# A two-layer graph kernel: TensorE issues in the order of the text, and the second layer multiplies by its weights before it mixes the nodes

## Chip, cores and metric

The kernel runs on one core of one Trainium2 chip. The metric is the device time of one execution in microseconds (us); the median of several runs counts. All data are float32.

## What is computed

There are 64 graphs (the batch) of 256 nodes with 512 features, and one 256 x 256 adjacency matrix for all of them. Layer 0 is masked attention with 8 heads of 64 features, layer 1 a graph attention with one head; both have a layernorm and a ReLU ahead of them and a residual around them.

```python
h = relu(layernorm(x))
q, k, v = h @ Wq + bq, h @ Wk + bk, h @ Wv + bv      # 8 heads of 64
scores = q k^T / 8 + (1 - adj) * -1e9                # per graph and head, 256 x 256
y = x + (softmax(scores) v) @ Wo + bo

h = relu(layernorm(y))
g = h @ W                                            # 512 x 512
s1, s2 = g @ a1, g @ a2                              # one number per node each
e = leaky_relu(s1[:, None] + s2[None, :], 0.2) * adj
out = y + elu(softmax(e) g + beta * g)
```

## The kernel before

Nodes lie on the 128 partitions in two tiles (`NT` = 2), features in four chunks of 128 (`DC` = 4), heads in four pairs (`NPAIR` = 4). Weights, mask and adjacency stay in SBUF. One pass of the main loop over `b` works on up to four graphs at once: the attention of graph `b`, the projections of graph `b+1`, the output projection and the second layer's scores of graph `b-1`, and the second layer's mixing and output of graph `b-2`. The text gives a priority to each step; which instruction an engine issues next was settled when the program was built, by a scheduler that may move steps past each other, and each engine then works through a fixed queue.

The steps that matter here, with the lines of the profile:

- `norm` and `norm_t` (lines 135 to 149 in their helpers): layernorm of `x`, then eight TensorE transposes (tile `tr_h`, two PSUM tiles of four), and a ReLU on the way back to SBUF, the first tile on VectorE (line 149) and the second on ScalarE (line 147).
- `project_qk` (line 184) fills one PSUM tile `qk` with a q chunk and a k chunk; VectorE takes q out (line 186), ScalarE then k (line 187). `project_v` (line 194) fills two tiles `pv`.
- `scores` (line 205): for a head pair, four matmuls with 64 rows of contraction into one tile `sc`, the heads on the two halves of the partitions. VectorE adds the mask (line 208) and takes the row maximum (line 214), ScalarE makes the exponentials with their sums (line 154), VectorE the reciprocal (line 156), GpSimd the product (line 216).
- `values`: eight transposes of the weights (tile `at`, line 163), copied to SBUF by ScalarE for the first head (line 165) and by VectorE for the second (line 167), then four matmuls (tile `av`, line 231) with 64 output columns per head: both node tiles of the first head, then both of the second. ScalarE copies the result (line 233).
- `project_o` (line 241, tiles `po`), the layernorm of `y`, with ReLU and without a transpose (line 252).
- `gat_scores`: VectorE multiplies `h` by the two vectors `W a1` and `W a2` and sums (line 262, four instructions), two small matmuls spread one of the sums over the partitions (tile `pe`, line 267); after the exponentials VectorE divides and adds `beta` on the diagonal (line 280).
- `gat_mix`: four transposes of the weights (tile `at_g`), and ((att + beta I) h) transposed, as eight matmuls of 256 columns (tiles `pz`, line 295). `gat_out`: that times W (tiles `pg`, line 307), then elu and the residual on ScalarE and VectorE, and the store.

A float32 matmul stands in the trace as two MATMUL instructions, each with its own weight load; a transpose stands as one. So `project_qk` of one chunk pair is eight matmuls and 16 instructions.

PSUM is held by three pools of two tiles each: `ps_sc` for `sc`, `ps_tr` for `at` and `at_g`, and `ps_mm` for all else (`tr_h`, `qk`, `pv`, `av`, `po`, `pe`, `pz`, `pg`). A tile of `ps_mm` can be filled only after one of the two before it has been copied out.

Of the kernel before, what the change touches and what calls it, by code (L numbers as in the profile page):

```python
# [14 lines left out]
P = 128  # L15
# [5 lines left out]
def kernel(ctx: ExitStack, tc: tile.TileContext, x, adj, wq, bq, wk, bk, wv, bv, wo, bo, w, a, beta, out):  # L21
# [23 lines left out]
    X, XN, HT, QT, KT, V, S, OT, Y, H2, ATT, ZT = ({} for _ in range(12))  # L45
# [48 lines left out]

    nc.vector.tensor_scalar(bo_sb, bo_sb, -1.0, None, ALU.add)

    diag = const.tile([P, NT, N], F32, name="diag")
    nc.gpsimd.memset(diag, 0.0)
    for t in range(NT):
        nc.vector.tensor_scalar(diag[:, t, t * P:(t + 1) * P], ident, beta_sb, None, ALU.mult)  # L100


    wa = const.tile([P, DC, 2], F32, name="wa")
    war = const.tile([P, 2, D], F32, name="war")

    def project_a():
        for j in range(2):
            aj = p2.tile([P, D], F32, tag="o", name=f"a_{j}")
            nc.sync.dma_start(aj, a[j * D:(j + 1) * D, 0].partition_broadcast(P))
            for c in range(DC):  # L110
                prod = p2.tile([P, D], F32, tag="t", name=f"prod_{j}_{c}")
                nc.vector.tensor_tensor(prod, w_sb[:, c, :], aj, ALU.mult)
                nc.vector.tensor_reduce(wa[:, c, j:j + 1], prod, AX.X, ALU.add)
            ps = ps_mm.tile([P, D], F32, tag="mm", name=f"war_{j}")
            for c in range(DC):
                nc.tensor.matmul(ps[:, c * P:(c + 1) * P], wa[:, c, j:j + 1].to_broadcast([P, P]), ident,
                                 start=True, stop=True)
            nc.vector.tensor_copy(war[:, j, :], ps)

    def statistics(src, name):  # L120

        st = p3.tile([P, NT, 6], F32, tag="st", name=f"st_{name}")
        mv = p3.tile([P, NT, 2], F32, tag="mv", name=f"mv_{name}")
        rstd = p3.tile([P, NT], F32, tag="rstd", name=f"rstd_{name}")
        for t in range(NT):
            nc.vector.bn_stats(st[:, t, :], src[:, t, :])
            nc.vector.bn_aggr(mv[:, t, :], st[:, t, :])
        nc.vector.tensor_scalar(rstd, mv[:, :, 1], EPS, None, ALU.add)
        nc.gpsimd.tensor_tensor(rstd, rstd, mhalf, ALU.pow)
        return mv, rstd  # L130

    def layernorm(src, name):

        mv, rstd = statistics(src, name)
        dst = p2.tile([P, NT, D], F32, tag="ln", name=f"ln_{name}")
# [15 lines left out]
    def exponents(e, rows, nmax, ssum):  # L151
# [4 lines left out]
        nc.vector.reciprocal(ssum, ssum)  # L156

# [42 lines left out]
    def scores(b, hp):  # L200
# [14 lines left out]
        exponents(rows, 2 * NT, nmax, ssum)  # L215
        nc.gpsimd.tensor_tensor(rows, rows, ssum.unsqueeze(2).to_broadcast([P, 2 * NT, N]), ALU.mult)  # L216
        S[b, hp] = s

    def values(b, hp):
        s = S.pop((b, hp))  # L220
        if hp == 0:
            OT[b] = p2.tile([P, NPAIR, N], F32, tag="oT", name=f"oT_{b}")
        sT = []
        for h in range(2):
            sT.append(p2.tile([P, NT, N], F32, tag="sT", name=f"sT_{b}_{hp}_{h}", bufs=4))
            transposed_weights(lambda t: s[:, h, t, :], sT[h], f"{b}_{hp}_{h}", (nc.scalar, nc.vector)[h])
        ps = ps_mm.tile([P, 512], F32, tag="mm", name=f"av_{b}_{hp}")
        for h in range(2):
            c0 = (2 * hp + h) * HD
            for k in range(NT):  # L230
# [5 lines left out]
    def project_o(b):  # L236
        Y[b] = p2.tile([P, NT, D], F32, tag="y", name=f"y_{b}", bufs=3)
        for t in range(NT):
            ps = ps_mm.tile([P, D], F32, tag="mm", name=f"po_{b}_{t}")
            for c in range(DC):  # L240
                nc.tensor.matmul(ps, OT[b][:, c, t * P:(t + 1) * P], wo_sb[:, c, :],  # L241
                                 start=(c == 0), stop=(c == DC - 1))
            nc.vector.tensor_tensor(Y[b][:, t, :], ps, X[b][:, t, :], ALU.add)
        for d in (OT, X, QT, KT, V):
            d.pop(b)

        mv, rstd = statistics(Y[b], f"y{b}")
        shift = p3.tile([P, NT], F32, tag="shift", name=f"shift_{b}")
        nc.vector.scalar_tensor_tensor(shift, mv[:, :, 0], -1.0, rstd, op0=ALU.mult, op1=ALU.mult)
        H2[b] = p2.tile([P, NT, D], F32, tag="h2", name=f"h2_{b}")  # L250
        for t in range(NT):
            nc.scalar.activation(H2[b][:, t, :], Y[b][:, t, :], AF.Relu, scale=rstd[:, t:t + 1],
                                 bias=shift[:, t:t + 1])


    def gat_scores(b):
        h2 = H2[b]
        s12 = p3.tile([P, 2, NT], F32, tag="s12", name=f"s12_{b}")
        for j in (1, 0):
            for t in range(NT):  # L260
                prod = p2.tile([P, D], F32, tag="t", name=f"sp_{b}_{j}_{t}")
                nc.vector.scalar_tensor_tensor(prod, h2[:, t, :], 1.0, war[:, j, :], op0=ALU.mult, op1=ALU.mult,  # L262
                                               accum_out=s12[:, j, t:t + 1])

        ps = ps_mm.tile([P, 512], F32, tag="mm", name=f"pe_{b}")
        for t in range(NT):
            nc.tensor.matmul(ps[:, t * P:(t + 1) * P], s12[:, 1, t:t + 1].to_broadcast([P, P]), ident,  # L267
                             start=True, stop=True)
        raw = p2.tile([P, NT, N], F32, tag="raw", name=f"raw_{b}")
        for t in range(NT):  # L270
            nc.scalar.activation(raw[:, t, :], ps[:, :N], AF.Identity, bias=s12[:, 0, t:t + 1])
# [6 lines left out]
        exponents(e, NT, nmax, ssum)  # L278
        for t in range(NT):
            nc.vector.scalar_tensor_tensor(e[:, t, :], e[:, t, :], ssum[:, t:t + 1], diag[:, t, :],  # L280
                                           op0=ALU.mult, op1=ALU.add)
        ATT[b] = e

    def gat_mix(b):

        e, h2 = ATT.pop(b), H2.pop(b)
        eT = p2.tile([P, NT, N], F32, tag="eT", name=f"eT_{b}")
        transposed_weights(lambda t: e[:, t, :], eT, f"g{b}", nc.vector)
        ZT[b] = p2.tile([P, DC, N], F32, tag="zT", name=f"zT_{b}")
        for i in range(2):  # L290
            ps = ps_mm.tile([P, 2, N], F32, tag="mm", name=f"pz_{b}_{i}")
            for j in range(2):
                c = 2 * i + j
                for k in range(NT):
                    nc.tensor.matmul(ps[:, j, :], h2[:, k, c * P:(c + 1) * P], eT[:, k, :],  # L295
                                     start=(k == 0), stop=(k == NT - 1))
            if i:
                nc.scalar.copy(ZT[b][:, 2:4, :], ps)
            else:
                nc.vector.tensor_copy(ZT[b][:, 0:2, :], ps)  # L300

    def gat_out(b):
        zT, y = ZT.pop(b), Y.pop(b)
        for t in range(NT):
            ps = ps_mm.tile([P, D], F32, tag="mm", name=f"pg_{b}_{t}")
            for c in range(DC):
                nc.tensor.matmul(ps, zT[:, c, t * P:(t + 1) * P], w_sb[:, c, :],  # L307
                                 start=(c == 0), stop=(c == DC - 1))
            m = p2.tile([P, D], F32, tag="t", name=f"m_{b}_{t}")
            nc.scalar.activation(m, ps, AF.Exp)  # L310
            nc.vector.scalar_tensor_tensor(m, m, 1.0, y[:, t, :], op0=ALU.min, op1=ALU.add)  # L311
            o = p2.tile([P, D], F32, tag="o", name=f"o_{b}_{t}")
            nc.vector.scalar_tensor_tensor(o, ps, 0.0, m, op0=ALU.max, op1=ALU.add)  # L313
            nc.sync.dma_start(out[b, t * P:(t + 1) * P, :], o)

    norm(0)
    norm_t(0)
    for d in range(DC):
        project_qk(0, d)
    project_v(0)  # L320
    scores(0, 0)
    project_a()

    for b in range(B + 2):
        prev, nxt = 0 <= b - 1 < B, b + 1 < B
        for hp in range(NPAIR):
            if b < B and hp + 1 < NPAIR:
                scores(b, hp + 1)
            if hp == 0:
                if b + 2 < B:  # L330
                    load(b + 2)
                if nxt:
                    norm(b + 1)
                if prev:
                    project_o(b - 1)
                if 0 <= b - 2 < B:
                    gat_mix(b - 2)
            elif hp == 1:
                if nxt:
                    norm_t(b + 1)  # L340
                    project_qk(b + 1, 0)
                    project_qk(b + 1, 1)
            elif hp == 2:
                if 0 <= b - 2 < B:
                    gat_out(b - 2)
                if prev:
                    gat_scores(b - 1)
                if nxt:
                    project_qk(b + 1, 2)
            else:  # L350
                if nxt:
                    project_qk(b + 1, 3)
                    project_v(b + 1)
                    scores(b + 1, 0)
            if b < B:
                values(b, hp)
# [29 lines left out]
```

## Time and profile before

| | us |
|---|---|
| median of 3 runs | 3751.84 (3750.86 to 3754.07) |
| the profiled execution's own time | 3754.07 |
| its span in the trace | 3752.3 |
| TensorE matmul busy | 3652.5 (97% of the span) |
| VectorE busy | 2137.2 (57%) |
| ScalarE busy | 1239.1 (33%) |
| GpSimd busy | 723.5 (19%) |
| share of the DMA engines in queue 1 | 5.7% |

The span runs from the first to the last instruction of the profiled execution; 1.8 us of its own time lie outside it, and this execution was 2.2 us over the median. "Busy" of TensorE counts matmuls from start to a modelled end, and they overlap, so the distance from one instruction's start to the next one's start (its pace) says more than its duration. The mean granted TensorE clock was 0.993. From the third pass of the loop on, the trace repeats itself every 57.76 us.

### The profile page before, as it was taken

To read this page: it belongs to the slowest core of one execution; us is meant where nothing else is said; L and a number is where in the kernel's file an instruction comes from. 1 tells how busy PE (TensorE), PEld (TensorE's weight loads), DVE (VectorE), ACT (ScalarE), POOL (GpSimd) and SP (SyncE) were. 2 spreads that over 40 slices of the span, in tenths; PEclk is the share of its full clock that TensorE was granted. 3 is DMA by queue.
4 is the path that set the end of the run, shared out by engine and by line. 5 is a ranking of instruction groups with operands and counts; after the bars stand their busy time and mean duration, and the time that the engine had idled before them with its cause. 6 is when DMAs were issued, how large, how long until landed. Compare 5 with 4: busy or idle time off the path is not lost.

```text
span 3752.3 us, 40118 instructions
## 1 busy us (share of the span) xinstructions
PE 3652.5 (97%) x15376; PEld 2288.7 (61%) x15376; DVE 2137.2 (57%) x3735; ACT 1239.1 (33%) x3585; POOL 723.5 (19%) x456
## 2 busy tenths in 40 slices
PE   8999999999999999999999999999999999999998
PEld 5666665666666656666566666665666656666664
DVE  5555555555555555555555555555555555555554
ACT  2333333333333333333333333333333333333332
POOL 2221121221211212212122121121221212212110
PEclk9999999999999999999999999999999999999999
DMA  2000000000000000000000000000000000000000
GB/s 99 12 20 20 17 17 17 23 17 18 17 21 19 17 17 20 20 17 17 17 23 17 18 17 23 17 17 17 23 17 17 18 17 23 17 18 17 17 12 17
DMA packets 40721, 76.24 MB, mean 20 GB/s; under 512 B 4433, under 2 KB 4689, under 8 KB 40529
## 3 DMA queue, kind: packets, MB, share of 16 engines
q1 hardware_dynamic: 40528, 73.68, 5.7%
q8 instruction: 121, 1.98, 0.2%
q14 instruction: 72, 0.58, 0.1%
HBM read 40.11 MB, written 33.55 MB: 20 GB/s over the span
## 4 chain that ended last, share of the span: by engine, by line
PE 84%; DVE 11%; ACT 4%; issue 0%; DMA 0%; POOL 0%; POOLq 0%; DVEq 0%; ACTq 0%
PE qk L184 25%; PE po L241 12%; PE pv L194 12%; PE sc L205 11%; PE av L231 9%; PE pz L295 6%; PE at L163 5%; DVE m L311 4%; ACT s L154 4%; DVE s L208 2%; DVE nmax L214 2%; PE tr_h L145 2%; PE pe L267 2%; DVE sp L262 1%; DVE o L313 1%; ACT m L310 1%
## 5 line engine op out<-in xcount | busy, mean ns | idle before, releaser
L216 POOL TENSOR_TENSOR s<-s,ssum 128x1024 f32<-128x1024 f32 x256 | 484.5, 1892 | 2742.2 <-DVE ssum L156 2694.1
L154 ACT ACTIVATE s<-s,nmax 128x256 f32<-128x256 f32 x1024 | 507.7, 497 | 683.0 <-DVE nmax L214 681.7
L208 DVE TENSOR_TENSOR s<-sc,mask 128x1024 f32<-128x1024 f32 x256 | 313.6, 1225 | 402.0 <-PE sc L205 402.0
L184 PE MATMUL qk<-hT,wq 128*128 128x256 f32 x2048 | 513.7, 395 | 2.1 <-ACT hT L147 1.6
L184 PE MATMUL qk<-hT,wk 128*128 128x256 f32 x2048 | 484.3, 379 | 0.0
L241 PE MATMUL po<-wo,oT 128*128 128x512 f32 x1024 | 456.8, 599 | 0.0
L307 PE MATMUL pg<-w,zT 128*128 128x512 f32 x1024 | 456.4, 598 | 0.0
L205 PE MATMUL sc<-kT,qT 64*128 64x256 f32 x2048 | 456.3, 422 | 0.0
L194 PE MATMUL pv<-wv,hT 128*128 128x512 f32 x1024 | 449.9, 592 | 0.0
L184 PEld LDWEIGHTS qk<-hT,wq 128*128 128x128 f32 x2048 | 385.3, 196 | 93.3 <-ACT sT L165 21.1
L184 PEld LDWEIGHTS qk<-hT,wk 128*128 128x128 f32 x2048 | 389.8, 190 | 53.4
L231 PE MATMUL av<-sT,v 128*64 128x256 f32 x2048 | 352.3, 392 | 2.7 <-ACT sT L165 1.5
L241 PEld LDWEIGHTS po<-wo,oT 128*128 128x128 f32 x1024 | 189.2, 190 | 235.5 <-issue 220.2
L307 PEld LDWEIGHTS pg<-w,zT 128*128 128x128 f32 x1024 | 189.4, 190 | 235.0 <-issue 234.8
L165 ACT COPY sT<-at 128x512 f32<-128x512 f32 x256 | 149.5, 584 | 551.3 <-PE at L163 551.1
L194 PEld LDWEIGHTS pv<-wv,hT 128*128 128x128 f32 x1024 | 194.6, 190 | 217.6 <-issue 214.3
L186 DVE TENSOR_SCALAR qT<-qk,bq 128x256 f32<-128x256 f32 x256 | 123.9, 484 | 345.9 <-PE qk L184 345.9
L205 PEld LDWEIGHTS sc<-kT,qT 64*128 64x128 f32 x2048 | 219.4, 185 | 154.9 <-issue 140.0
L214 DVE TENSOR_REDUCE nmax<-s 128x4 f32<-128x1024 f32 x256 | 311.2, 1216 | 4.3
L163 PE MATMUL at<-ident,s 128*128 128x128 f32 x2048 | 299.9, 275 | 0.9 <-POOL s L216 0.9
L163 PEld LDWEIGHTS at<-ident,s 128*128 128x128 f32 x2048 | 240.5, 141 | 96.3 <-issue 87.8
L231 PEld LDWEIGHTS av<-sT,v 128*64 128x64 f32 x2048 | 172.8, 136 | 142.6 <-issue 53.4
(63 smaller groups left out, 3299.2 us busy)
## 6 DMA issues: line engine op xcount, KB each, us to landing
x<-in_x_dram SPq DMA_DIRECT2D x64, 512.0 KB, 3.7
out_dram<-o SPq DMA_DIRECT2D x128, 256.0 KB, 2.0
wq<-in_L_gnn_Wq_dram SPq DMA_DIRECT2D x1, 1024.0 KB, 6.5
wk<-in_L_gnn_Wk_dram SPq DMA_DIRECT2D x1, 1024.0 KB, 9.1
wv<-in_L_gnn_Wv_dram SPq DMA_DIRECT2D x1, 1024.0 KB, 7.5
wo<-in_L_gnn_Wo_dram SPq DMA_DIRECT2D x1, 1024.0 KB, 9.1
w<-in_L_gnn_W_dram SPq DMA_DIRECT2D x1, 1024.0 KB, 11.4
a<-in_L_gnn_a_dram SPq DMA_DIRECT2D x2, 256.0 KB, 10.2
```

What stands on the lines that cost most here:

```text
L154: nc.scalar.activation(e[:, r, :], e[:, r, :], AF.Exp, bias=nmax[:, r:r + 1], accum_out=ssum[:, r:r + 1])
L163: nc.tensor.transpose(ps[:, k, t * P:(t + 1) * P], e(t)[:, k * P:(k + 1) * P], ident)
L184: nc.tensor.matmul(ps[:, j, :], wj[:, c, d * P:(d + 1) * P], HT[b][:, c, :], start=(c == 0), stop=(c == DC - 1))
L194: nc.tensor.matmul(ps, HT[b][:, c, t * P:(t + 1) * P], wv_sb[:, c, :], start=(c == 0), stop=(c == DC - 1))
L205: nc.tensor.matmul(ps[:, h, t, :], QT[b][hs, hp, t * P:(t + 1) * P], KT[b][hs, hp, :], start=True, stop=True)
L208: nc.vector.tensor_tensor(s.rearrange("p h t k -> p h (t k)"), ps.rearrange("p h t k -> p h (t k)"), mask.rearrange("p t k -> p (t k)").un ...
L214: nc.vector.tensor_reduce(nmax, rows, AX.X, ALU.max, negate=True)
L216: nc.gpsimd.tensor_tensor(rows, rows, ssum.unsqueeze(2).to_broadcast([P, 2 * NT, N]), ALU.mult)
L231: nc.tensor.matmul(ps[h * HD:(h + 1) * HD, :N], V[b][:, k, c0:c0 + HD], sT[h][:, k, :], start=(k == 0), stop=(k == NT - 1))
L241: nc.tensor.matmul(ps, OT[b][:, c, t * P:(t + 1) * P], wo_sb[:, c, :], start=(c == 0), stop=(c == DC - 1))
L295: nc.tensor.matmul(ps[:, j, :], h2[:, k, c * P:(c + 1) * P], eT[:, k, :], start=(k == 0), stop=(k == NT - 1))
L307: nc.tensor.matmul(ps, zT[:, c, t * P:(t + 1) * P], w_sb[:, c, :], start=(c == 0), stop=(c == DC - 1))
```

## The change

TensorE's queue now follows the text: the main part stands inside a manual schedule for that engine, and the loop body is written out as the list in which TensorE is to work. The other engines are still scheduled at build time. `values` is split into `weights_t` (the transposes and their copies) and `values` (the matmuls), with other work between the two; the matmuls of `values` alternate between the heads. The score matmuls of a head pair, which alternated before, stay together.

The second layer is evaluated in another order. The layernorm of `y` is now transposed as that of `x` is (`gat_norm_t`, tiles `tr_g`, eight transposes), and `gat_h` makes g = h W (tiles `ph`, 16 instructions of 512 columns, copied to SBUF by ScalarE). The two score terms come from the transposed `h` on TensorE: `W a2`, spread over 128 columns (`wa2b`), gives one term with four matmuls of 256 columns, and eight matmuls with a single moving column give the other. The weights are divided on GpSimd, as in layer 0, without the diagonal. `gat_out` needs two matmuls of 512 columns per tile; beta times g is added by VectorE, and elu takes two passes on ScalarE and three on VectorE. `project_a` and the constants lose what is not needed any more.

```diff
-        for h in range(2):
-            c0 = (2 * hp + h) * HD
-            for k in range(NT):
+        for k in range(NT):
+            for h in range(2):
+                c0 = (2 * hp + h) * HD
                 nc.tensor.matmul(ps[h * HD:(h + 1) * HD, :N], V[b][:, k, c0:c0 + HD], sT[h][:, k, :],
                                  start=(k == 0), stop=(k == NT - 1))
...
+    def gat_norm_t(b):
+        H2T[b] = p2.tile([P, DC, N], F32, tag="h2T", name=f"h2T_{b}")
+        transposed_relu(YN.pop(b), H2T[b], f"g{b}")
+        HS[b] = p2.tile([P, NT, D], F32, tag="hs", name=f"hs_{b}")
+    def gat_h(b, t):
+        ps = ps_mm.tile([P, D], F32, tag="mm", name=f"ph_{b}_{t}")
+        for c in range(DC):
+            nc.tensor.matmul(ps, H2T[b][:, c, t * P:(t + 1) * P], w_sb[:, c, :],
+                             start=(c == 0), stop=(c == DC - 1))
+        nc.scalar.copy(HS[b][:, t, :], ps)
     def gat_scores(b):
...
+        for c in range(DC):
+            nc.tensor.matmul(ps[:, :N], wa2b[:, c, :], h2T[:, c, :], start=(c == 0), stop=(c == DC - 1))
+        for t in range(NT):
+            for c in range(DC):
+                nc.tensor.matmul(ps[:, N + t:N + t + 1], h2T[:, c, t * P:(t + 1) * P], wa[:, c, 0:1],
                                  start=(c == 0), stop=(c == DC - 1))
...
     def gat_out(b):
...
-            for c in range(DC):
-                nc.tensor.matmul(ps, zT[:, c, t * P:(t + 1) * P], w_sb[:, c, :],
-                                 start=(c == 0), stop=(c == DC - 1))
+            for k in range(NT):
+                nc.tensor.matmul(ps, eT[:, k, t * P:(t + 1) * P], hs[:, k, :],
+                                 start=(k == 0), stop=(k == NT - 1))
+            nc.vector.scalar_tensor_tensor(g, hs[:, t, :], beta_sb, ps, op0=ALU.mult, op1=ALU.add)
-            nc.scalar.activation(m, ps, AF.Exp)
+            nc.scalar.activation(m, g, AF.Relu, scale=-1.0)
+            nc.scalar.activation(m, m, AF.Exp, scale=-1.0)
...
+    with tc.manual_schedule(engines={mybir.EngineType.PE}):
```

The order of TensorE's queue in one full pass (`b` the graph whose attention is worked on), as the built program has it:

| graph b | graph b+1 | graph b-1 | graph b-2 |
|---|---|---|---|
| sc 1 | | po 0 | |
| at 0 | | po 1 | at_g |
| av 0 | tr_h 0, 1 | | pg 0, 1 |
| sc 2 | qk 0 | | |
| at 1 | qk 1 | | |
| av 1, sc 3 | | tr_g 0, 1 | |
| | qk 2 | | |
| at 2 | | ph 0 | |
| av 2 | | ph 1, pe, 16 single-column instructions | |
| | sc 0 | | |
| at 3 | qk 3 | | |
| av 3 | pv 0, 1 | | |

Rows follow each other, and within a row TensorE goes from left to right. Of the two PSUM tiles of `ps_mm`, pg 0 takes the one that tr_h 0 filled and pg 1 that of tr_h 1; qk 2 takes that of tr_g 1, ph 0 that of tr_g 0, pv 0 that of qk 3, and av 3 that of `pe`. VectorE's queue in the same pass has, behind the scores of graph b-1, this order: copy of s1, leaky ReLU, product with adj, mask of sc 0 (b+1), row maximum of e, row maximum of sc 0, copy of at 3 (second head), reciprocals, q of qk 3. ScalarE's has: two `raw`, copy of at 3 (first head), exponentials of e, exponentials of sc 0, k of qk 3, copy of av 3.

## The prediction

> **What bounds the kernel now.** I read the page first. TensorE is busy 97% of the span, and 84% of the chain that ended last lies on it.
>
> ```profile
> PE 3652.5 (97%) x15376; PEld 2288.7 (61%) x15376; DVE 2137.2 (57%) x3735; ACT 1239.1 (33%) x3585; POOL 723.5 (19%) x456
> PE 84%; DVE 11%; ACT 4%; issue 0%; DMA 0%; POOL 0%; POOLq 0%; DVEq 0%; ACTq 0%
> ```
>
> So TensorE's queue sets the time: what it issues, at what pace, and what it waits for. The waits, next, show one real wait of it in each batch:
>
> ```profile
> PE pe L267 <- DVE sp L262: 72.1, 64, 1.8
> ```
>
> For the pace I take the timeline of TensorE in the middle of the run: start, length of the group, line, tiles, count. A group's cost is the distance to the next group's start, since lengths overlap.
>
> ```profile
> 1800.98 7.03 PE L194 MATMUL pv<-wv,hT 128*128 128x512 f32 x16
> ...
> 1811.45 7.13 PE L241 MATMUL po<-wo,oT 128*128 128x512 f32 x16
> 1818.42 0.60 PE L163 MATMUL at_g<-ident,e 128*128 128x128 f32 x4
> ...
> 1820.02 3.72 PE L295 MATMUL pz<-eT,h 128*128 128x256 f32 x16
> 1823.58 0.60 PE L163 MATMUL at<-ident,s 128*128 128x128 f32 x4
> 1824.15 1.89 PE L231 MATMUL av<-sT,v 128*64 128x256 f32 x8
> 1825.97 0.70 PE L205 MATMUL sc<-kT,qT 64*128 64x256 f32 x4
> 1826.60 1.09 PE L145 MATMUL tr_h<-ident,ln_x 128*128 128x128 f32 x8
> ...
> 1836.23 1.09 PE L231 MATMUL av<-sT,v 128*64 128x256 f32 x8
> 1837.25 1.13 PE L205 MATMUL sc<-kT,qT 64*128 64x256 f32 x6
> 1838.31 7.13 PE L307 MATMUL pg<-w,zT 128*128 128x512 f32 x16
> 1845.28 0.93 PE L163 MATMUL at<-ident,s 128*128 128x128 f32 x7
> 1847.33 0.49 PE L267 MATMUL pe<-ident,s 128*128 128x128 f32 x2 [1.13 <-DVE sp L262]
> ```
>
> The next pv begins at 1858.73, 57.75 us later: the batch's period (57.76 on average). Single instructions inside these groups start 0.429 us apart for 512 columns, 0.216 for 256, 0.109 for a transpose. The same eight av instructions cost 1.02 us at 1836.23 and 1.82 at 1824.15, where the copies of the transposed weights came late; a piece of four sc costs 0.63, of six 1.06, and the unbroken eight of the prologue (at 33.80) also 1.06.
>
> [...] an `at` is followed after 0.202 us by an sc instead of 0.109, the last sc or av of a group takes 0.306 instead of 0.216, and the first full-array instruction after it 0.104 more (0.056 for a transpose). [...] in the av at 1836.23 the second head's first matmul, queued behind four instructions of the first head, starts 13 ns after that head's first. So the heads already overlap, and alternating them in the text buys nothing by itself.
>
> **The change, part by part, per batch.** *Taken off TensorE:* pz 16 x 0.216 = 3.46; half of pg, 8 x 0.429 = 3.43; the two old pe with their wait, 0.74 + 1.29. Scores: nine pieces cost 6.57, four unbroken groups 4 x 1.064 = 4.26: -2.32. Values: the four groups cost 1.82 + 1.28 + 2 x 1.02 = 5.15; with other matmuls between transposes and values all can run at 1.02: -1.06. Mode changes around the groups, counted in both lists: -0.10. Together -12.40. *Added:* ph 16 x 0.429 = 6.86; the new pe 8 x 0.216 = 1.73; tr_g 8 x 0.109 = 0.87; 16 single-column instructions, which the trace does not show. Each loads 128 weight columns, [...] not over the 0.213 that the old pe takes from first to second instruction with its load exposed; I take the load-bound pace of the transposes, 0.109: 1.74. Together +11.21. Work alone: 57.76 - 12.40 + 11.21 = 56.57, a gain of 1.19.
>
> *Waits added.* TensorE may no longer slip other work in, so each late copy stops all behind it. I laid the batch out along the fixed queues with these durations (mean ns of one):
>
> ```profile
> L154 ACT ACTIVATE s<-s,nmax 128x256 f32<-128x256 f32 x800 | 396.7, 497 | 541.0 <-DVE nmax L214 541.0
> L216 POOL TENSOR_TENSOR s<-s,ssum 128x1024 f32<-128x1024 f32 x200 | 378.5, 1892 | 2168.2 <-DVE ssum L156 2168.2
> L208 DVE TENSOR_TENSOR s<-sc,mask 128x1024 f32<-128x1024 f32 x200 | 245.0, 1225 | 322.6 <-PE sc L205 322.6
> L311 DVE SCALAR_TENSOR_TENSOR m<-m,y 128x512 f32<-128x512 f32 x100 | 149.6, 1496 | 15.1 <-ACT m L310 15.1
> L149 DVE TENSOR_SCALAR hT<-tr_h 128x512 f32<-128x512 f32 x50 | 34.0, 681 | 0.0
> L147 ACT ACTIVATE hT<-tr_h 128x512 f32<-128x512 f32 x50 | 29.9, 599 | 64.2 <-PE tr_h L145 64.2
> ```
>
> From TensorE coming free to the reader's start the trace has 0.20 us, from a copy's end to TensorE 0.05; independent neighbours on VectorE or ScalarE overlap by 0.09.
> 1. pg 0 needs the PSUM tile of tr_h 0: 0.20 + 0.68 + 0.04 = 0.92 after tr_h 0, covered by tr_h 1 alone (0.44): 0.48. Before, transposes and scores stood behind tr_h.
> 2. qk 2 needs the tile of tr_g 1, straight ahead of it: 0.20 + 0.60 + 0.05 = 0.85, no cover.
> 3. av 3 needs the second head's copy on VectorE, queued behind graph b-1's second-layer scores. From pe's end: s1 0.41, two `raw` on ScalarE 0.91, leaky ReLU 0.73, product 0.60, mask of sc 0 1.14, maximum of e 0.60, maximum of sc 0 1.14, the copy with its landing 0.72: 6.25. Cover: sc 0 1.06, at 3 0.93, qk 3 3.55: 5.54. Wait 0.71.
> 4. pv 0 needs qk 3's tile; its k copy stands on ScalarE behind the four exponentials of sc 0 (1.99, 0.49 apart). They start 5.66 after pe's end, the copy takes 0.52: 8.17. Cover 5.54 + 0.71 + 1.02 = 7.27. Wait 0.90.
> 5. Behind waits 1 and 2 the weight load cannot run ahead: 2 x 0.104 = 0.21.
>
> Sum 3.15. Period 56.57 + 3.15 = 59.72, against 57.76: +1.96.
>
> *At no cost:* softmax chains have 14 us or more of other matmuls (about 7.5 needed); the layernorm of y 16 us (about 7). VectorE loses four products and the division and gains copies and elu steps, and stays near 60%; ScalarE gains two copies and two passes. GpSimd gains the second layer's product (about 0.95, half of 1.89), between graphs' softmax products, with 12 us to spare. SP's loads and stores are the same in number and size, and queue 1 moves in 5.7% of the time. One cover is thin: av 1 has 0.34 us to spare behind the elu, mask and exponentials of sc 2. [...] the trace shows an `m` (line 311) lasting 2.31 us instead of 0.69, ending 0.55 after a GpSimd product. The new elu step meets GpSimd's addition to x (2.35 us). That costs 0 to 0.1; if the layernorm scaling is caught too, 0.7.
>
> **The sum.** The profiled execution's span is 3752.3. Its 61 full batches: 61 x 1.96 = +119.6. Ends, laid out the same way: the prologue loses the matmuls that spread a (line 116) but must keep the text's order, about -1.5. The second pass lacks only at_g and pg (3.9), so 55.8; before it lacked pz and a longer pg too, and took 47.3 from po to po: +8.5. The pass of the last graph, without graph b+1, 38.5 against 35.4: +3.1. From the last po on: po 7.0, at_g with its copy and pg 4.9, tr_g with its copies 1.8, ph 6.9, pe 3.5, the score chain to the product 5.9, at_g with copy 1.4, pg 3.4, last elu, store and end 7.4, so 42.2 against 47.1: -4.9. Together +5.2. Every fifth or sixth batch has 1.64 us at half TensorE clock; I leave it. 3752.3 + 124.8 = 3877.1; with 1.8 outside the span 3878.9 for that execution, and 2.2 less on the median: 3876.7.
>
> **Rivals.** *The copies keep ahead.* With the same two `ps_mm` tiles the profile of before has scarcely a wait of TensorE but pe's, which speaks for readers that are always in time. With 0.5 us of waits left per batch the period would be 57.07: 61 x -0.69 + 5.2 gives 3715. It decides for faster once the waits sum to under 1.1 us (1.19 less the ends' 5.2 / 61). Against it: before, other matmuls stood between tr_h and the next user of its tile, and waits 1 and 2 alone make 1.33 out of measured durations. *VectorE is later still*[...]: av 1 waits 0.7 more, 61 x 0.7 = 43, 3919. *The single-column instructions expose their loads* (0.213): +1.66 a batch, 3978. *The change does not do what it says:* for the values this holds, as said, and is in the sum.
>
> **Chances.** Forecast (3825 to 3905) 0.60; [...] exposed loads 0.09; faster 0.07; balance within 0.2% (7.5 us, about what a measurement of this kernel can tell from no change) 0.04. Slower is 0.60 + 0.20 + 0.09 = 0.89. The range 3825 to 3950 leaves out faster, balance and exposed loads, 0.20.
>
> **What would show it.** The period between two pv should be 59.7; sc groups of eight at 1.06, av at 1.02; single-column starts 0.109 apart; TensorE idle ahead of pg (released by VectorE hT), qk 2 (ScalarE h2T), av 3 (VectorE sT) and pv 0 (ScalarE kT). I am wrong if those idle times are under half of what I list, or if others as large appear.

## The result and the profile after

| | before | after |
|---|---|---|
| median | 3752.76 (3750.86 to 3754.07, 4 runs) | 3856.97 (3856.38 to 3857.76, 4 runs) |
| ratio, 95% interval | | 1.0278 [1.026, 1.0296] |
| the profiled execution's own time | 3754.07 | 3856.66 |
| its span | 3752.3 | 3854.9 |
| period in the middle of the run | 57.76 | 59.53 |

The change costs 2.8%. The page's first part and its chain, after:

```profile
PE 3707.5 (96%) x16640; PEld 2315.6 (60%) x16640; DVE 1945.2 (50%) x3347; ACT 1284.8 (33%) x3713; POOL 789.7 (20%) x519
PE 83%; DVE 9%; ACT 7%; issue 1%; DMA 0%; POOL 0%; POOLq 0%; ACTq 0%; DVEq 0%
```

TensorE still sets the time: 96% busy, 83% of the chain. What is new is in its waits. The columns are engine, tile and line that waited, what it waited for, us in total, times, longest:

```profile
PE pv L177 <- ACT kT L170: 52.9, 63, 0.9
PE qk L167 <- ACT h2T L129: 42.5, 62, 0.7
PE pg L282 <- DVE hT L131: 14.8, 61, 0.2
```

The wait for VectorE's `sp`, 72.1 us in 64 times, is gone; three others stand there once in every batch, each for a copy that empties a PSUM tile. They are longer than this list says, because the ends of matmuls are modelled. The timeline of TensorE shows their true size as the distance from one start to the next:

```profile
1797.00 7.13 PE L177 MATMUL pv<-wv,hT 128*128 128x512 f32 x16 [0.85 <-ACT kT L170]
1804.06 1.13 PE L188 MATMUL sc<-kT,qT 64*128 64x256 f32 x8
1805.12 3.70 PE L228 MATMUL po<-wo,oT 128*128 128x512 f32 x8
...
1813.50 1.08 PE L218 MATMUL av<-sT,v 128*64 128x256 f32 x8
1814.52 1.20 PE L127 MATMUL tr_h<-ident,ln_x 128*128 128x128 f32 x8
1815.96 3.70 PE L282 MATMUL pg<-hs,eT 128*128 128x512 f32 x8 [0.24 <-DVE hT L131]
...
1830.71 1.10 PE L127 MATMUL tr_g<-ident,ln_y 128*128 128x128 f32 x8
1832.49 1.99 PE L167 MATMUL qk<-hT,wq 128*128 128x256 f32 x8 [0.69 <-ACT h2T L129]
...
1846.73 1.84 PE L256 MATMUL pe<-wa,h2T 128*128 128x1 f32 x16
1848.50 1.13 PE L188 MATMUL sc<-kT,qT 64*128 64x256 f32 x8
...
1854.05 1.63 PE L218 MATMUL av<-sT,v 128*64 128x256 f32 x8
1856.53 5.85 PE L177 MATMUL pv<-wv,hT 128*128 128x512 f32 x13 [0.85 <-ACT kT L170]
```

From pv to pv are 59.53 us, in every batch. The unbroken sc group costs 1.06, an av in time 1.02. The places with waits:

- tr_h to pg: 1.44, where eight transposes take 0.93: a wait of 0.51.
- tr_g to qk 2: 1.78 less 0.93: 0.85.
- av 3 to pv: 2.48. Of this 1.02 is av's own work; between the last av instruction and the first pv lie 1.23 where 0.31 is usual, so 0.92 is pv's wait; the remaining 0.54 is inside the group, where the second head waits for its copy.
- The first instruction of pg takes 0.533 where 0.429 is usual, and that of qk 2 takes 0.320 for 0.216: two weight loads of 0.104 that could not run ahead.

Together 3.03 us a batch.

### The profile page after: what moved, and what is told of

Same layout as the page of the kernel before. It is cut to its first block, busy times and chain, and to the rows that moved or that the text cites. A ratio compares the mean times of both kernels' runs of the same rounds, so it can differ in the third digit from the quotient of the medians.

```text
span 3854.9 us, 42334 instructions
## 1 busy us (share of the span) xinstructions
PE 3707.5 (96%) x16640; PEld 2315.6 (60%) x16640; DVE 1945.2 (50%) x3347; ACT 1284.8 (33%) x3713; POOL 789.7 (20%) x519
## 4 chain that ended last, share of the span: by engine, by line
PE 83%; DVE 9%; ACT 7%; issue 1%; DMA 0%; POOL 0%; POOLq 0%; ACTq 0%; DVEq 0%
PE qk L167 18%; PE ph L245 12%; PE po L228 12%; PE pv L177 12%; PE pg L282 6%; PE sc L188 5%; PE av L218 5%; PE at L146 4%; ACT s L136 3%; PE pe L253 3%; PE pe L256 3%; DVE s L191 2%; DVE nmax L197 2%; PE tr_g L127 2%; ACT raw L262 1%; DVE e L264 1%
## 5 line engine op out<-in xcount | busy, mean ns | idle before, releaser
L167 PE MATMUL qk<-hT,wq 128*128 128x256 f32 x2048 | 499.1, 387 | 43.2 <-ACT h2T L129 42.5
L177 PE MATMUL pv<-wv,hT 128*128 128x512 f32 x1024 | 456.5, 598 | 52.9 <-ACT kT L170 52.9
L245 PE MATMUL ph<-w,h2T 128*128 128x512 f32 x1024 | 467.0, 599 | 1.0 <-DVE h2T L131 1.0
L167 PEld LDWEIGHTS qk<-hT,wq 128*128 128x128 f32 x2048 | 369.9, 190 | 119.7 <-ACT h2T L129 57.2
L218 PE MATMUL av<-sT,v 128*64 128x256 f32 x2048 | 315.0, 395 | 6.5 <-DVE sT L150 4.1
L245 PEld LDWEIGHTS ph<-w,h2T 128*128 128x128 f32 x1024 | 184.4, 190 | 209.7 <-issue 184.1
L179 DVE TENSOR_TENSOR v<-pv,bv 128x512 f32<-128x512 f32 x128 | 88.6, 692 | 420.8 <-PE pv L177 420.8
L188 PE MATMUL sc<-kT,qT 64*128 64x256 f32 x2048 | 291.1, 403 | 0.0
L146 PE MATMUL at<-ident,s 128*128 128x128 f32 x2048 | 269.9, 275 | 6.8 <-POOL s L139 6.8
L139 POOL TENSOR_TENSOR e<-e,gsum 128x512 f32<-128x512 f32 x64 | 66.5, 1039 | 1011.8 <-DVE gsum L138 1011.8
L188 PEld LDWEIGHTS sc<-kT,qT 64*128 64x128 f32 x2048 | 176.8, 186 | 133.8 <-issue 121.3
## 6 DMA issues: line engine op xcount, KB each, us to landing
w<-in_L_gnn_W_dram SPq DMA_DIRECT2D x1, 1024.0 KB, 11.6
```

Of the source, the lines that this page charges most:

```text
L139: nc.gpsimd.tensor_tensor(e, e, ssum.unsqueeze(2).to_broadcast([P, rows, N]), ALU.mult)
L146: nc.tensor.transpose(ps[:, k, t * P:(t + 1) * P], e(t)[:, k * P:(k + 1) * P], ident)
L167: nc.tensor.matmul(ps[:, j, :], wj[:, c, d * P:(d + 1) * P], HT[b][:, c, :], start=(c == 0), stop=(c == DC - 1))
L177: nc.tensor.matmul(ps, HT[b][:, c, t * P:(t + 1) * P], wv_sb[:, c, :], start=(c == 0), stop=(c == DC - 1))
L188: nc.tensor.matmul(ps[:, h, t, :], QT[b][hs, hp, t * P:(t + 1) * P], KT[b][hs, hp, :], start=True, stop=True)
L218: nc.tensor.matmul(ps[h * HD:(h + 1) * HD, :N], V[b][:, k, c0:c0 + HD], sT[h][:, k, :], start=(k == 0), stop=(k == NT - 1))
```

## Experiments

The theory: what costs the time is not the amount of work but four copies that stand late in the queues of VectorE and ScalarE while TensorE, tied to the text, has nothing to put in their place; the second layer's new evaluation eats what the fixed order gains. Rivals: the fixed order in itself is the loss; or the single-column instructions are; or the alternating heads are.

### 1. The new text, TensorE's queue built as before (e1_sched)

```diff
-    with tc.manual_schedule(engines={mybir.EngineType.PE}):
+    with ExitStack():
```

> The changed kernel with the manual schedule taken off TensorE: the new second layer and the split of transposes and values stay, but the build's scheduler orders TensorE again. Theory (the loss is the new layer's work plus copies that come late, not the fixed order as such): the built queue puts half of the transposes at 2 between tr_g and qk 2 (covers about 0.65 of wait 2) and a piece of scores between tr_h and pg (covers about 0.3 of wait 1, but costs 0.4 in mode changes); waits 3 and 4 stay. So 0.5 to 0.7 us less per batch, about 3815 to 3830. Rival (the fixed order is the culprit): back to the time of before, about 3750, or under it.

Measured 3802.67, ratio to before 1.0134 [1.0117, 1.0151], some 12 us under what was expected. In the list of TensorE's waits one that comes in each batch is left:

```profile
PE pv L177 <- ACT kT L170: 13.7, 62, 0.2
```

So the built queue fills part of the waits, but breaks groups to do it (the sc around pg into pieces of 2 and 6, those around pv into 4 and 4, six of eight `at` instructions put between tr_g and qk 2): the period falls by only 0.78, from 59.53 to 58.75. Read from start to start, 1.03 us of waits are still there: 0.54 inside av 3, 0.30 ahead of pv and 0.20 ahead of qk 2. "Mode changes", here as in the prediction, are the steps between groups of unlike tile shape, which the trace of before shows longer than those within a group (0.202 for 0.109 from `at` to sc, 0.306 for 0.216 behind an sc). The 0.4 for them was the author's estimate: here the piece of 2 ahead of pg takes 0.62 and that of 6 behind it 1.06, as much as eight in one piece. The fixed order is 54 us of the loss. How the rest divides between the second layer and these waits, this run does not show; sections 2 and 6 do.

### 2. The old second layer under a fixed order (e2_old_layer_fixed, e8_old_layer_fixed_2, e11_fixed_heads_alternate)

The kernel before, with `values` split into transposes and matmuls as in the change, and its loop written out as one list for TensorE:

```diff
-        for hp in range(NPAIR):
...
+    with tc.manual_schedule(engines={mybir.EngineType.PE}):
...
+            if nxt:
+                project_qk(b + 1, 2)
+            if prev:
+                gat_scores(b - 1)
+            if now:
+                values(b, 2)
+            if nxt:
+                scores(b + 1, 0)
+            if now:
+                weights_t(b, 3)
```

> The kernel before with its own second layer, but with TensorE in a fixed order like that of the change (transposes early, values later, score groups unbroken, heads alternating), and with transposes or scores behind each pair of PSUM tiles that is copied out. Theory: TensorE's work is the 57.76 us of before less scores 2.32, values 1.06, the wait for pe 1.29 and 0.1 of mode changes, so 53.0; with 0.3 to 0.8 of waits left the period is 53.3 to 53.8, the time about 3465 to 3500. Rival (a fixed order brings waits of some 3 us wherever it is put): 56 us, about 3640. Rival (the order gains nothing, the heads overlapped before): about 3750.

In this kernel the heads in fact follow each other, as in the kernel before; they do not alternate, other than the expectation says. Measured 3552.05, 0.9467 [0.9453, 0.9481]: far faster, and yet 52 us over the top of what was expected. The list of waits names the reason, beside 22.1 us in 61 times of qk 2 for `o`:

```profile
PE av L236 <- ACT kT L187: 68.1, 62, 1.1
```

av 2 waits 1.10 us for the k copy of qk 2. In the list only `pe` lies between the two, 0.6 us of work, and VectorE has the four `sp` products ahead of the q copy. ScalarE's k copy follows it. No other work covers the two. Moved behind the next graph's scores and at 3, av 2 has cover (e8):

```diff
             if prev:
                 gat_scores(b - 1)
-            if now:
-                values(b, 2)
             if nxt:
                 scores(b + 1, 0)
             if now:
                 weights_t(b, 3)
+                values(b, 2)
```

> The old second layer in a fixed order, as in the run that did so, with one move: the scores of the next graph and the transposes at 3 stand ahead of av 2 instead of behind it. There av 2 waited 1.10 us for the k copy of qk 2, whose tile it takes, with only the small pe between. Theory: 1.93 us of cover takes that wait away, 62 x 1.1 = 68 less, about 3484, with the 0.35 at qk 2 left. Rival (VectorE is what is late there, so the wait moves to av 3 or pv 0): 3530 to 3550.

Measured 3493.92, 0.9312 [0.9298, 0.9326]. The av wait is gone from the list of waits; that of qk 2 for `o` remains as it was, 22.1 us in 61 times. The period is 53.73, 4.03 under the kernel before. The prediction's own terms give 2.32 (unbroken scores) + 1.06 (values) + 1.29 (the pe wait) + 0.10 (mode changes) = 4.77, and `pe` in one piece costs 0.54 instead of 0.74. Against that stand two waits with the loads behind them, again from start to start: 0.63 at qk 2 and 0.36 at qk 0. That makes 3.98, close to what was measured. The text of `scores` is the same in all these kernels; what is worth 2.32 is that the list keeps its eight instructions together, where the built queue had cut the four groups into nine pieces. So a fixed order is no loss in itself; with the old layer it is worth 6.9%. This version beats both kernels.

e11 is e8 with the heads alternating in `values`:

```diff
-        for h in range(2):
-            c0 = (2 * hp + h) * HD
-            for k in range(NT):
+        for k in range(NT):
+            for h in range(2):
+                c0 = (2 * hp + h) * HD
```

> The old second layer in the better fixed order, with the value matmuls alternating between the heads; the run before it kept them one head after the other. Theory: all four groups already run at 1.02 us there, so the time stays at 3494 within 0.2%. Rival (alternating saves or costs slots): over 10 us of difference.

Measured 3494.25, 0.9311 [0.9297, 0.9325], with a period of 53.70 for 53.73. Where the copies are in time, alternating is worth nothing, since the heads overlapped already: in e8, where TensorE's queue is the text with one head after the other, the first instructions of the two heads of an av start 13 or 14 ns apart.

### 3. The kernel before, only the heads alternating (e10_only_heads_alternate)

The edit is that of e11, made in the kernel before, with the queue built as there.

> The kernel before with one edit: the value matmuls alternate between the heads; the scheduler still orders TensorE. Theory (the heads overlap anyhow, as the starts 13 ns apart in the trace show): within 0.2% of before, 3746 to 3761; if anything changes, the group that waited for the second head's copy (1.82 us) loses its head start and gains at most 0.3 us, 20 in all. Rival (alternating is what lets the halves of the array work together): 1.06 less a batch, about 3685.

Measured 3821.08, 1.0182 [1.0167, 1.0197]: no change had been expected, and it costs 67.5 us. First the kernel before, where an av stands among scores:

```profile
2039.50 0.70 PE L205 MATMUL sc<-kT,qT 64*128 64x256 f32 x2
2040.13 1.36 PE L231 MATMUL av<-sT,v 128*64 128x256 f32 x8
2041.42 1.13 PE L205 MATMUL sc<-kT,qT 64*128 64x256 f32 x6
2042.47 7.13 PE L241 MATMUL po<-wo,oT 128*128 128x512 f32 x16
```

And the same place in e10:

```profile
2016.32 0.70 PE L205 MATMUL sc<-kT,qT 64*128 64x256 f32 x2
2016.95 0.65 PE L231 MATMUL av<-sT,v 128*64 128x256 f32 x2
2017.52 0.70 PE L205 MATMUL sc<-kT,qT 64*128 64x256 f32 x2
2018.15 1.08 PE L231 MATMUL av<-sT,v 128*64 128x256 f32 x6
2019.16 0.70 PE L205 MATMUL sc<-kT,qT 64*128 64x256 f32 x4
2019.79 7.13 PE L241 MATMUL po<-wo,oT 128*128 128x512 f32 x16
...
2058.28 3.68 PE L184 MATMUL qk<-hT,wq 128*128 128x256 f32 x8
```

The second matmul of the group is now the second head's, whose copy comes later, and the queue as built has a score in between. From the first sc to po are 3.47 us instead of 2.97: the av costs 0.57 + 1.01 for 1.29, and the scores 3 x 0.63 for 0.63 + 1.05, because in this window a piece of two instructions costs as much as one of four. At av 0 the same happens (3.38 for 3.03 from its last transposes to tr_h). Together 0.85 a batch; the period rose from 57.76 to 58.60, which over 61 batches is 51 us. The last line above is the rest: those eight instructions last 3.68 where 1.99 is usual; the granted TensorE clock is 0.50 there. Such stretches stand in 19 batches of e10 and in 10 of the kernel before (mean granted clock 0.988 and 0.993), 1.6 to 1.7 us each, so some 15 us more.

### 4. Without the single-column instructions (e3_no_single_column)

It leaves out the 16 instructions of `gat_scores` that give s1; s1 is read from two columns of the other term instead.

```diff
-        for t in range(NT):
-            for c in range(DC):
-                nc.tensor.matmul(ps[:, N + t:N + t + 1], h2T[:, c, t * P:(t + 1) * P], wa[:, c, 0:1],
-                                 start=(c == 0), stop=(c == DC - 1))
...
-        nc.vector.tensor_copy(s1, ps[:, N:N + NT])
+        nc.vector.tensor_copy(s1, ps[:, N - NT:N])
```

> The changed kernel without its 16 single-column instructions: one of the second layer's two score terms is not computed (two columns of the other are read in its place). Theory: they cost their weight loads, 1.77 us a batch, and nothing hides them: 64 x 1.77 = 113 less, about 3744. Rival (their loads would run ahead under neighbours, and the time goes into the waits behind them): under 40 less, about 3820.

Measured 3748.54, 0.9989 [0.9981, 0.9998]: 108.4 us less than after, 1.69 for each of 64 graphs. These 16 instructions with eight products of 128 x 128 by one column cost as much as eight instructions with 256 columns: each brings its own weights, and both the loads and the matmuls follow each other 0.112 us apart. They alone are as large as the whole loss, but so are the waits: neither is the one cause.

### 5. The waits covered one by one (e5_tr_g_covered, e6_scores_earlier, e7_tr_h_swapped)

e5 puts at 2 between tr_g and qk 2:

```diff
-            if nxt:
-                project_qk(b + 1, 2)
             if now:
                 weights_t(b, 2)
+            if nxt:
+                project_qk(b + 1, 2)
```

> The changed kernel with one move in TensorE's text: the transposes at 2 (0.87 us) stand between tr_g and qk 2 instead of behind qk 2. Theory (wait 2 is the ScalarE copy of the second tr_g tile, 0.85 without cover): the wait of qk 2 and the load behind it, 0.95 us a batch, go and nothing else changes, 62 x 0.95 = 59 less, about 3798. Rival (the time comes back as a later wait, at ph 0 or av 2): under 20 less, about 3840 to 3855.

Measured 3802.22, 1.0133 [1.0116, 1.015]. The wait of qk 2 has left the list, and those of pv (52.9 us) and pg (14.7) stand as they did. 54.8 us in 62 batches are 0.88. That is the wait of 0.85, but not all of the 0.95 expected: the weight load behind it stays exposed, and qk 2's first instruction still takes 0.297 instead of 0.216.

e6 puts the first scores of the next graph ahead of ph 1 and `pe`, so that their mask, maximum and exponentials are past when the copies of at 3 and the k of qk 3 are due:

```diff
+            if nxt:
+                scores(b + 1, 0)
             if prev:
                 gat_h(b - 1, 1)
                 gat_scores(b - 1)
-            if nxt:
-                scores(b + 1, 0)
```

> The changed kernel with one move: the scores of the next graph (sc 0) stand ahead of ph 1, pe and the single-column instructions instead of behind them, so that VectorE and ScalarE have them behind them before the second layer's scores come. Theory (waits 3 and 4 are queueing behind the second layer's scores): 1.46 us of waits at av 3 and pv 0 fall to 0.1 to 0.2, about 62 x 1.3 = 81 less, 3776. Rival (the second layer's own exponentials then hold k of qk 3 back): 0.8 left, 40 less, about 3816.

Measured 3768.50, 1.0042 [1.0027, 1.0057]. Of both waits at the end of the batch only 0.13 ahead of pv is left, and those of qk 2 (42.6 us) and pg (14.7) stand. 88.5 us in 62 batches are 1.43, for 0.54 + 0.92 read from the trace.

e7 tries the same for pg, with the transposes of tr_h ahead of av 0:

```diff
-            if now:
-                values(b, 0)
             if nxt:
                 norm_t(b + 1)
+            if now:
+                values(b, 0)
```

> The changed kernel with one move: tr_h stands ahead of av 0 instead of behind it. Av 0 (1.02 us) would cover the copy for pg, but av 0 itself takes the PSUM tile of the second tr_h. Theory (what waits is whoever fills the next tile, not the reader of hT): the wait of 0.5 ahead of pg goes and one of 0.85, without cover, appears ahead of av 0; 0.2 to 0.3 us more a batch, about 3870. Rival (the wait is for the data hT): 0.5 less a batch, about 3825.

Measured 3874.74, 1.0325 [1.0309, 1.034], slower than after by 17.8 as expected: av 0 takes the next PSUM tile instead, and so takes over the wait: in the list, pg's is gone, and av waits for ScalarE's `hT`, 41.9 us in 61 times. The wait belongs to whoever fills a tile of `ps_mm` first behind the transposes; swapping two fillers only renames it.

### 6. The moves together (e9_two_moves, e4_waits_covered, e12_tr_h_later)

e9 is e5's and e6's edits in one kernel.

> The changed kernel with the two moves that helped alone: transposes at 2 behind tr_g, and the next graph's scores ahead of ph 1 and pe. Theory (the waits are independent): the two gains add, 54.8 + 88.5 = 143 less than the changed kernel, about 3714, under the time of before; left are the 0.5 us ahead of pg. Rival (one move's gain holds back the other's): 3730 to 3768.

Measured 3713.70, 0.9895 [0.9879, 0.9912]. 54.8 + 88.5 = 143.3, and the kernel is 143.3 faster than after: the waits are independent, and the two moves turn the changed kernel from 2.8% slower into 1.1% faster than before. Of the waits that come in each batch the list has one left:

```profile
PE pg L282 <- DVE hT L131: 14.7, 61, 0.2
```

The period of 57.23 still is 3.50 over that of e8, with about as much waiting left in both (0.8 and 1.0, exposed loads included). The prediction's prices for the layer alone make 11.21 for what was added, less 3.46 + 3.43 for pz and half of pg and 0.54 for the old pe: 3.8. That is about the price of the new evaluation on TensorE.

e4 adds a third move, which was to cover pg's wait with at 1:

```diff
-            if nxt:
-                norm_t(b + 1)
             if last:
                 gat_out(b - 2)
...
             if now:
                 scores(b, 2)
             if nxt:
-                project_qk(b + 1, 0)
+                norm_t(b + 1)
             if now:
                 weights_t(b, 1)
+            if nxt:
+                project_qk(b + 1, 0)
```

> The changed kernel with TensorE's text in another order, the same instructions: the transposes at 2 ahead of qk 2 (wait 2), tr_h behind the scores sc 2 and ahead of the transposes at 1 (wait 1), and the scores of the next graph ahead of ph 1 and pe (waits 3 and 4). Theory: the four waits shrink from 2.9 to 0.1 to 0.3 us and their load exposure goes, the period falls to 56.6 to 56.9, the time to about 3680 to 3700, under that of before. Rival (the waits move to other places, the work itself is longer than laid out): 58 to 59, about 3770 to 3820.

Measured 4178.83, 1.1136 [1.112, 1.1153], nearly 500 us off. In the list of waits stands a new one, qk 0 for the copy of tr_h, 342.5 us in 62 times. The timeline ahead of it, VectorE's lines with GpSimd's addition:

```profile
2029.69 2.37 POOL L155 TENSOR_TENSOR x<-x,bo 128x1024 f32<-128x1024 f32 x1 [2.03 <-DVE ln_x L119]
...
2030.18 2.42 DVE L291 SCALAR_TENSOR_TENSOR o<-g,m 128x512 f32<-128x512 f32 x1
...
2033.25 1.22 DVE L191 TENSOR_TENSOR s<-sc,mask 128x1024 f32<-128x1024 f32 x1
...
2034.38 0.68 DVE L291 SCALAR_TENSOR_TENSOR o<-g,m 128x512 f32<-128x512 f32 x1
...
2036.71 0.68 DVE L131 TENSOR_SCALAR hT<-tr_h 128x512 f32<-128x512 f32 x1
```

VectorE has its own queue. With tr_h later in the text, the copy `hT` comes to stand behind four elu steps, the mask and the maximum, and qk 0 cannot start without it. One of these steps lasts 2.42 beside GpSimd's addition instead of 0.68. That is not all; for behind the wait TensorE is at about half pace, as the TensorE lines of the same kernel show:

```profile
2037.54 3.75 PE L167 MATMUL qk<-hT,wq 128*128 128x256 f32 x8 [5.63 <-DVE hT L131]
2041.08 2.52 PE L167 MATMUL qk<-hT,wk 128*128 128x256 f32 x8
```

3.54 from first to second start, where 1.83 is usual. Over the whole span the mean granted clock is 0.947, against 0.997 in the changed kernel. e12 makes this third move alone, as a test of the reading:

> The changed kernel with the one move that is left of the four-wait version: tr_h behind the scores sc 2 and ahead of the transposes at 1. In the version with all moves qk 0 waited 5.6 us a batch for VectorE's copy of tr_h, which the build had put behind the mask, row maximum and elu steps, and the TensorE clock was half for some 6 us after it. Theory (this move alone does that, the others do not matter): the changed kernel's 3857 plus what the four-wait version lost against the two good moves, 4179 - 3714 = 465, so about 4320. Rival (it takes the moves together): under 3950.

Measured 4318.13, 1.1506 [1.1489, 1.1523], with the same wait (342.4 us in 62 times) beside those of pv and qk 2. The third move alone does the harm.

## Why the prediction held

Forecast 3876.7, measured 3856.97: in the range, on the predicted side, for the predicted reasons, and 20 us too high. For the profiled execution the forecast was 3878.9 and its own time 3856.66, 22.2 less. By the prediction's own terms:

| term | predicted | measured |
|---|---|---|
| wait 1, pg behind tr_h | 0.48 | 0.51 |
| wait 2, qk 2 behind tr_g | 0.85 | 0.85 |
| wait 3, av 3 | 0.71 | 0.54 |
| wait 4, pv 0 | 0.90 | 0.92 |
| exposed loads | 0.21 | 0.21 |
| 16 single-column instructions | 1.74 | 1.77 |
| period | 59.72 | 59.53 |
| ends | +5.2 | +11.0 |
| half-clock stretches | left as they were | none in the batches |

*Work.* 59.53 less 3.03 of waits are 56.50, for 56.57 predicted. That this lies 1.26 under the old period does not mean fewer or shorter matmuls: the old period holds 1.29 of waiting for `sp`, and without it is 56.47. What unbroken scores and values in time save, the new layer takes up again. Confirmed is also the price of 0.109 for a single-column instruction (0.112 in the trace), which was to be no more than 0.213; in the trace of before the transposes of a group start 0.109 apart, and so, for the most part, do their loads.

*Waits.* All four stand where they were put, each released by the copy that was named; e5 and e6 take three of them away for the sum that was read. Wait 3 is 0.17 smaller than its term, and the trace shows where: counted from the start of sc 0, the second head's matmuls start after 6.10 instead of 6.25, because the two `raw` start after 0.30 (0.41 predicted) and take 0.87 (0.91); the cover is 5.54 as predicted. That the first head starts ahead of this copy gains nothing. From the second head's first instruction to the end of the group are 1.01, and so they are in the kernel before, where at 1824.15 the second head starts 0.81 behind the first.

*Period.* 0.19 less, over 61 batches 11.6 us less.

*Ends.* +11.0 instead of +5.2, so 5.8 us more. The first po starts at 83.22 for 81.02 before (+2.2; -1.5 was predicted), where the fixed list has TensorE wait 6.84 for graph 0's first softmax; from inside this wait on the granted clock is 0.50 for 10.24. The second pass takes 55.1 (55.8 predicted). That of the last graph takes 40.7 (38.5 predicted): without the next graph's projections, av 1 waits 3.21 for its second copy, and from inside this wait on the granted clock is 0.50 for 6.83. From the last po on it is 44.7 (42.2 predicted), and the same stretch of the kernel before is 49.0, where the prediction had 47.1: it had not counted the first two po instructions, which run ahead of the last av.

*The term that failed.* "Every fifth or sixth batch has 1.64 us at half TensorE clock; I leave it." Before, 10 batches had such a stretch: 16.4 us. After, no batch has one, and all periods are 59.52 or 59.53. The prediction gave no reason for leaving the term as it was; the stretches of the kernel before start 1.9 to 2.2 us behind the end of the wait for `sp`, which the change takes away. With the period and the ends this is -16.4 - 11.6 + 5.8 = -22.2, the whole difference of the profiled execution.

*Rivals.* "The copies keep ahead" needed waits under 1.1 and they are 3.03; e9, whose period is only 0.73 over the 56.50 of work, lands at 3713.70, close to the 3715 that the rival gave for 0.5 of waits. "The single-column instructions expose their loads" is out by the 0.112. "VectorE later still", with 0.20 of the chances, did not come about in the changed kernel (av 1 there takes 1.02); its 0.7 was the author's estimate. But e4 shows how near it was: one step moved, and VectorE's queue costs 5.63 a batch. "The change does not do what it says" holds for the values (e11).

## What to carry to other kernels

When one engine's queue is fixed by hand, list for every PSUM tile the copy that frees it, add up what stands ahead of that copy on its own engine, and put at least that much other matmul work between filling the tile and filling it again; the sum of four such shortfalls, 2.8 us a batch, outweighed all that the change saved. Judge an order and a new algorithm apart: here an order whose copies have cover was worth 6.9% with the old layer and the new evaluation cost 3.5 us a batch, and the two together looked like one bad change. Before moving a step, ask where its copy will come to stand in the other engines' queues: in e4 and e12 the build moved the copy along with the text, behind VectorE's elu steps.

## What the runs showed of the hardware beyond that

The half-clock stretches come at regular distances. In the clock records of the kernel before, the granted TensorE clock is 0.50 for 3.413 us in each stretch of the batches, and the stretches start 348.2 us apart, 102.0 times 3.413 (once 406.2, 119.0 times). In e10 most are 177.5 apart (52.0 times). In both kernels each costs 1.6 to 1.7, half of 3.413. In e4 they come once a batch, 64.85 apart (19.0 times), and last 6.83, twice 3.413, with a wait of 5.63 in each batch. At the two ends of the changed kernel, stretches of 10.24 and 6.83 start inside waits of 6.84 and 3.21.

Before and e10 have no wait longer than 1.14 in a batch. Their stretches follow the wait for `sp`, where small pieces and idle time alternate for some 4 us; the changed kernel, with waits up to 0.92 in dense work, has no stretch in its batches. Most batches of the kernel before have that wait and no stretch. What makes the clock fall these runs do not show.
